# Attention scores in two float32r terms, and exponentials over three PSUM banks, in a convolution-and-attention kernel

## The chip, the core and the metric

The kernel runs on one core of a Trainium2 chip. The core has five engines that this text names: TensorE (PE in the profile; PEld is its weight load), VectorE (DVE), ScalarE (ACT), GpSimd (POOL) and SyncE (SP), which here only issues DMAs. Matmuls write to PSUM, which has eight banks of 512 float32 columns on 128 partitions; the other engines work from SBUF and PSUM.

The metric is device time in microseconds (us) of one execution. Before the change it is 10433.82 us, the median of three runs (10430.26 to 10446.56).

## What is computed

Two layers are applied to four images of 64 x 64 pixels with 128 channels. The part that matters here is the attention of the second layer ("layer 1"): per image 4096 tokens, 16 heads of 8 channels, no mask.

```python
q = (x @ wq).reshape(bsz, seqlen, N_HEADS, HEAD_DIM)
k = (x @ wk).reshape(bsz, seqlen, N_HEADS, HEAD_DIM)
v = (x @ wv).reshape(bsz, seqlen, N_HEADS, HEAD_DIM)
scores = jnp.einsum('bqhd,bkhd->bhqk', q, k)
probs = jax.nn.softmax(scores.astype(jnp.float32), axis=-1).astype(q.dtype)
attn = jnp.einsum('bhqk,bkhd->bqhd', probs, v).reshape(bsz, seqlen, DIM)
h = x + attn @ wo
```

Around it stand, in layer 0, two 3 x 3 convolutions and a causal attention with one small head, and after it in layer 1 a gated feed-forward network and a mixture of eight experts. All of it is float32, and the scores must keep nearly float32 accuracy.

## The kernel before

The four images are done one after another (L681). For each: convolutions (`l0_convs`), layer 0's attention (`l0_attention`), the transposed input `yT`, `l1_attention`, then `l1_ffn` and `l1_experts` over eight blocks of 512 tokens.

**Layer 1's attention** (L430 to L564) is written by hand in the order in which TensorE is to do it; the tile framework puts in the waits. It has two parts.

*Preparation* (L435 to L464). For each of eight column blocks of 512 tokens two matmuls make the queries and the keys in one PSUM tile. `three_terms` (L234) splits these float32 numbers into three bfloat16 terms whose sum is the number: ScalarE rounds the first term (L238), VectorE takes the rest (L239), GpSimd rounds the second (L240), VectorE takes the third (L241). The terms go out to DRAM (L444, L445), since they must come back in another order of partitions. Values `v1` are made at L453 to L463.

*The main loop* (L517 to L563). Heads are done in four groups `g` of four heads; a head has its own group ("slot") of 32 SBUF partitions. For each group and each block `c` of 512 queries (128 such pairs over the four images) there are 32 tiles `kt` of 128 keys. For each key tile:

- Scores (L546). The keys `kx` lie with 8 channels x 3 terms = 24 rows in each slot, and the queries `qx` hold, for each query term i, that term repeated on the 24 rows. So three matmuls of 24 rows, added up in PSUM, give all nine products of terms. Four heads times three terms are 12 matmuls, for four banks: two score tiles `s` of 1024 columns. There are three such tiles (L103), in six banks.
- Exponentials (L556). ScalarE turns each score tile into an SBUF tile `e` of 1024 columns, from a pool of eight.
- Accumulation (L509), two key tiles late (`LAG`). For each head one float32 matmul of a 128 x 9 weight (a one for the softmax's sum, and 8 value channels) adds to `acc`, the head's 32 partitions of one further bank. The trace records each of these float32 matmuls as two.

After the last key tile VectorE copies `acc` to SBUF (L524), and in the next block, after its second key tile, `by_token` transposes and divides it (L495 to L500); the transposes have the eighth bank.

Keys are loaded for a whole group (L474) into one of two buffers, queries for a block (L483) into one of two, both one ahead. All these DMAs are issued by SP in program order.

The pools that the change touches serve other stages too: the score tiles and `e` tiles are used by the convolutions, layer 0's attention (scores L402, exponentials L415 and L418, accumulation L381), the feed-forward network (L583 to L587) and the experts (L666, L675).

Of the kernel before, what the change touches and what calls it, by code (L numbers as in the profile page):

```python
# [8 lines left out]

FP = mybir.dt.float32  # L10
BF = mybir.dt.bfloat16
AF = mybir.ActivationFunctionType
ALU = mybir.AluOpType
AX = mybir.AxisListType

P = 128
C = 128
IMG = 64
N = IMG * IMG
NT = N // P  # L20
QB = 512
NQ = N // QB
# [4 lines left out]
SLOT = 32  # L27
NSLOT = P // SLOT
# [5 lines left out]
HIDDEN = 344  # L34
FCH = [(0, 128), (128, 128), (256, 88)]
NE = 8

NTERM = 3  # L40
# [49 lines left out]
def fast_path(ctx: ExitStack, tc: tile.TileContext, a: dict, where: dict, out: bass.AP, verdict):  # L90
# [2 lines left out]
    x = a["x"]  # L93
    B = x.shape[0]
    LAG = 2

    const = ctx.enter_context(tc.tile_pool(name="f_const", bufs=1))
    big = ctx.enter_context(tc.tile_pool(name="f_big", bufs=1))
    ep = ctx.enter_context(tc.tile_pool(name="f_ep", bufs=8))
    wk = ctx.enter_context(tc.tile_pool(name="f_wk", bufs=2))  # L100
    sm = ctx.enter_context(tc.tile_pool(name="f_sm", bufs=2))
    dram = ctx.enter_context(tc.tile_pool(name="f_dram", bufs=2, space=bass.MemoryType.DRAM))
    ps_s = ctx.enter_context(tc.tile_pool(name="f_ps_s", bufs=3, space=bass.MemoryType.PSUM))  # L103
    ps_o = ctx.enter_context(tc.tile_pool(name="f_ps_o", bufs=1, space=bass.MemoryType.PSUM))
    ps_m = ctx.enter_context(tc.tile_pool(name="f_ps_m", bufs=1, space=bass.MemoryType.PSUM))

    def s_tile():
        return ps_s.tile([P, 1024], FP, tag="s", name="s")

    def m_tile():  # L110
        return ps_m.tile([P, QB], FP, tag="m", name="m")

    def e_tile():
        return ep.tile([P, 1024], FP, tag="e", name="e")


    n_fast = where["head_sum"][1]
# [311 lines left out]

    def l1_attention(b, yT, h):  # L430

        d_k = dram.tile([P, NTERM, N], BF, tag="k1", name="d_k1")
        d_q = dram.tile([NQ, P, NTERM, QB], BF, tag="q1", name="d_q1")
        top = sm.tile([P, 2, NQ], FP, tag="top", name="top")
        for c in range(NQ):  # L435
            cols = slice(c * QB, (c + 1) * QB)
            ps = s_tile()
            nc.tensor.matmul(ps[:, :QB], lhsT=wq1, rhs=yT[:, cols], start=True, stop=True)
            nc.tensor.matmul(ps[:, QB:], lhsT=wk1, rhs=yT[:, cols], start=True, stop=True)
            nc.vector.tensor_reduce(  # L440
                top[:, :, c], ps.rearrange("p (j n) -> p j n", j=2), AX.X, ALU.max, apply_absolute_value=True
            )
            terms = three_terms(ps)
            nc.sync.dma_start(out=d_k[:, :, cols], in_=terms[:, :, QB:])  # L444
            nc.sync.dma_start(out=d_q[c], in_=terms[:, :, :QB])  # L445

        tops = sm.tile([P, 2], FP, tag="tops", name="tops")
        nc.vector.tensor_reduce(tops, top, AX.X, ALU.max)
        nc.vector.tensor_tensor(seen[:, 2, b : b + 1], tops[:, 0:1], tops[:, 1:2], ALU.mult)
        nc.vector.tensor_scalar(seen[:, 2, b : b + 1], seen[:, 2, b : b + 1], 1e30, None, ALU.min)  # L450

# [12 lines left out]
        nc.vector.tensor_reduce(seen[:, 3, b : b + 1], top_v, AX.X, ALU.max)  # L464


        rows = HD1 * NTERM

        def keys(g):
            kx = big.tile([P, N], BF, tag="kx", bufs=2, name="kx")  # L470
            for j in range(NSLOT):
                head = NSLOT * g + j
                src = d_k[head * HD1 : (head + 1) * HD1].rearrange("d y n -> (d y) n")
                nc.sync.dma_start(out=kx[j * SLOT : j * SLOT + rows, :], in_=src)  # L474
            return kx

        def queries(g, c):

            qx = wk.tile([P, NTERM, QB], BF, tag="qx", name="qx")
            for j in range(NSLOT):  # L480
                head = NSLOT * g + j
                src = d_q[c][head * HD1 : (head + 1) * HD1].rearrange("d x n -> d (x n)")
                nc.sync.dma_start(  # L483
                    out=qx[j * SLOT : j * SLOT + rows].rearrange("p x n -> p (x n)"),
                    in_=src.unsqueeze(1).to_broadcast([HD1, NTERM, NTERM * QB]),
                )
            return qx

        nt = big.tile([P, NT, C], FP, tag="y", name="nt")

        def by_token(g, c, at):

            ps = m_tile()
            for k in range(4):
                nc.tensor.transpose(ps[:, k * P : (k + 1) * P], at[:, k * P : (k + 1) * P], ident)  # L495
# [11 lines left out]
        def add_up(g, c, kt, es):  # L507
            for j in range(NSLOT):
                nc.tensor.matmul(  # L509
                    acc[j * SLOT : j * SLOT + 1 + HD1, :],  # L510
                    lhsT=v1[:, kt, NSLOT * g + j, :],
                    rhs=es[j // 2][:, (j % 2) * QB : (j % 2 + 1) * QB],
                    start=kt == 0,
                    stop=kt == NT - 1,
                )

        order = [(g, c) for g in range(NG1) for c in range(NQ)]  # L517
        ready = []

        def finish(n, kt, es):  # L520
            add_up(*order[n], kt, es)
# [7 lines left out]
        kx, qx = keys(0), queries(0, 0)  # L529
        kx_next = qx_next = None  # L530
        late = []
        for n, (g, c) in enumerate(order):
            if n:
                qx = qx_next
                if c == 0:
                    kx = kx_next
            if n + 1 < len(order):
                qx_next = queries(*order[n + 1])
            if c == 0 and g + 1 < NG1:
                kx_next = keys(g + 1)  # L540
            for kt in range(NT):
                ss = [s_tile(), s_tile()]
                for i in range(NTERM):
                    for j in range(NSLOT):
                        r = slice(j * SLOT, j * SLOT + rows)
                        nc.tensor.matmul(  # L546
                            ss[j // 2][:, (j % 2) * QB : (j % 2 + 1) * QB],
                            lhsT=kx[r, kt * P : (kt + 1) * P],
                            rhs=qx[r, i, :],
                            start=i == 0,  # L550
                            stop=i == NTERM - 1,
                        )
                es = []
                for ps in ss:
                    e = e_tile()
                    nc.scalar.activation(e, ps, AF.Exp)  # L556
                    es.append(e)
                late.append((n, kt, es))
                if len(late) > LAG:
                    finish(*late.pop(0))  # L560
        for item in late:
            finish(*item)
        by_token(*order[-1], ready.pop())  # L563
        return nt  # L564

# [847 lines left out]
```

## Time and profile before

| | |
|---|---|
| median of three runs | 10433.82 us |
| the profiled execution | 10433.93 us |
| its span, first to last instruction | 10432.1 us |
| mean granted TensorE clock | 0.966 |
| TensorE busy | 9972.6 us (96%) |
| ScalarE busy | 8198.4 us (79%) |
| VectorE busy | 1150.2 us (11%) |
| GpSimd busy | 184.3 us (2%) |

The profile is one execution taken by the hardware profiler. In its list of costliest groups a row gives the line, engine and operation, what is written from what, the shapes and the count; then the busy time in all, the mean time of one in ns, and the idle time of the engine just before them with what ended it. Busy time counts overlapping instructions of an engine once, so a group's busy time can be less than its count times its mean. Ends of matmuls are modelled, and a busy TensorE may be one that waits. The chain of waits follows the work that ended last backwards, from each instruction to what released it. A table of stretches gives, for each stretch, the busy time and count of each engine, the granted clock, and the DMA share and rate. A timeline lists start, length, engine, line and count of merged instructions.

### The profile page before, as it was taken

The numbers are of one execution on the slowest core, as the hardware profiler recorded it, in microseconds if no ns is written. First come the engines' busy times: TensorE is split into PE (matmuls) and PEld (weight loads), VectorE is DVE, ScalarE is ACT, GpSimd is POOL, SyncE is SP. The second block draws the span as 40 slices with busy tenths as digits, with TensorE's granted clock in tenths as the row PEclk, the third lists the DMA queues.
The fourth block names the chain that finished last, engine by engine and source line by source line (L and its number), as shares of the span: only waits on it lengthen the run. The fifth ranks groups of instructions, "written<-read, shape, count | busy, mean of one in ns | idle before, by whom it ended". The sixth has DMA issues, their size and how long they took to land.

```text
span 10432.1 us, 204188 instructions
## 1 busy us (share of the span) xinstructions
PE 9972.6 (96%) x90561; PEld 3179.9 (30%) x90565; DVE 1150.2 (11%) x3539; ACT 8198.4 (79%) x8965; POOL 184.3 (2%) x177
## 2 busy tenths in 40 slices
PE   8899999997989999999798999999979899999997
PEld 4322222224432222222442222222244222222224
DVE  1200000004220000000412000000051200000005
ACT  1699999991169999999116999999911799999991
POOL 0000000000000000000000000000000000000000
PEclk9999999998999999999889999999988999999998
DMA  1100000000010000000001000000000100000000
GB/s 26 35 6 10 6 9 7 6 5 15 5 34 6 10 6 9 7 6 5 16 4 35 7 9 6 10 6 6 5 16 4 35 7 9 6 10 6 6 5 9
DMA packets 86914, 112.51 MB, mean 11 GB/s; under 512 B 8835, under 2 KB 71779, under 8 KB 84195
## 3 DMA queue, kind: packets, MB, share of 16 engines
q1 hardware_dynamic: 83267, 97.59, 3.2%
q8 instruction: 710, 11.63, 0.5%
q10 hardware_dynamic: 2752, 1.77, 0.1%
q14 instruction: 185, 1.52, 0.0%
HBM read 64.99 MB, written 34.34 MB: 10 GB/s over the span
## 4 chain that ended last, share of the span: by engine, by line
PE 93%; DVE 4%; DMA 1%; ACT 1%; issue 0%; SPq 0%; POOL 0%; DVEq 0%; ACTq 0%; POOLq 0%
PE acc L509 38%; PE s L546 35%; PE s L291 5%; PE s L276 2%; PE s L666 2%; PE acc L381 2%; DVE t L675 2%; PE s L402 1%; PE s L583 1%; PE s L584 1%; PE m L495 1%; PE m L592 1%; PE m L231 1%; PE s L367 1%; PE m L574 0%
## 5 line engine op out<-in xcount | busy, mean ns | idle before, releaser
L556 ACT ACTIVATE e<-s 128x1024 f32<-128x1024 f32 x8192 | 7642.7, 1022 | 149.5 <-PE s L546 149.5
L509 PE MATMUL acc<-e,f_v 128*9 128x512 f32 x32768 | 4296.2, 595 | 4.5 <-ACT e L556 4.5
L546 PE MATMUL s<-qx,kx 24*128 24x512 bf16 x49152 | 3926.0, 377 | 29.5 <-DMA kx<-d_k 28.5
L546 PEld LDWEIGHTS <-kx 24*128 24x128 bf16 x49152 | 1548.0, 91 | 3823.5 <-issue 3467.2
L509 PEld LDWEIGHTS acc<-e,f_v 128*9 128x9 f32 x32768 | 486.7, 88 | 1753.4 <-issue 1687.1
L524 DVE COPY at<-acc 128x512 f32<-128x512 f32 x128 | 88.6, 692 | 7149.6 <-PE acc L509 7149.6
L291 PE MATMUL s<-c,f_w2c 128*128 128x512 f32 x1152 | 499.9, 592 | 0.0
L666 PE MATMUL s<-f_we,e 128*128 128x512 f32 x512 | 313.1, 763 | 58.2 <-DVE t L675 53.2
L299 ACT ACTIVATE e<-s,f_b 128x512 f32<-128x512 f32 x32 | 22.0, 687 | 422.8 <-PE s L291 422.7
L675 DVE SCALAR_TENSOR_TENSOR t<-s,gate,t 128x128 f32<-128x128 f32 x1024 | 305.9, 343 | 5.3 <-PE s L666 2.5
L291 PEld LDWEIGHTS s<-c,f_w2c 128*128 128x128 f32 x1152 | 215.5, 189 | 263.5 <-issue 263.5
L418 ACT ACTIVATE e<-s 128x1024 f32<-128x1024 f32 x224 | 217.6, 1021 | 91.1 <-PE s L402 90.4
L276 PE MATMUL s<-e,f_w1c 128*128 128x512 f32 x576 | 249.9, 596 | 3.1 <-DVE t L675 1.9
L402 PE MATMUL s<-qk 36*128 36x512 bf16 (+1 forms) x576 | 169.3, 388 | 76.0 <-DMA qk<-d_q 74.1
L655 ACT COPY g<-m 8x512 f32<-8x512 f32 x32 | 18.4, 575 | 230.4 <-PE m L653 230.4
L232 ACT COPY e<-m 128x512 f32<-128x512 f32 x64 | 37.5, 586 | 204.4 <-PE m L231 204.4
L381 PE MATMUL acc<-e,f_v 128*17 128x512 f32 (+3 forms) x1152 | 197.7, 600 | 0.0
L586 ACT ACTIVATE e<-s 128x512 f32<-128x512 f32 (+1 forms) x96 | 56.8, 596 | 165.6 <-PE s L584 165.5
L588 POOL TENSOR_TENSOR t<-t,h 128x512 f32<-128x512 f32 x32 | 40.5, 1266 | 8117.7 <-DVE h L577 8117.7
L666 PEld LDWEIGHTS s<-f_we,e 128*128 128x128 f32 x512 | 118.7, 247 | 202.9 <-issue 120.9
L283 ACT ACTIVATE c<-s,f_b 128x1024 f32<-128x1024 f32 x16 | 17.9, 1118 | 186.7 <-PE s L276 186.7
L276 PEld LDWEIGHTS s<-e,f_w1c 128*128 128x128 f32 x576 | 109.2, 190 | 141.7 <-issue 141.0
(146 smaller groups left out, 2962.0 us busy)
## 6 DMA issues: line engine op xcount, KB each, us to landing
qx<-d_q SPq DMA_DIRECT2D x512, 72.0 KB
d_k<-x SPq DMA_DIRECT2D x32, 384.0 KB
d_q<-x SPq DMA_DIRECT2D x32, 384.0 KB
kx<-d_k SPq DMA_DIRECT2D x64, 192.0 KB
t<-in_x_dram SPq DMA_DIRECT2D x16, 512.0 KB
out_dram<-t SPq DMA_DIRECT2D x32, 256.0 KB
f_w2c<-in_L_conv_W_dram ACTq DMA_DIRECT2D x1, 1152.0 KB
qk<-d_q SPq DMA_DIRECT2D x12, 96.0 KB
```

Of the source, the lines that this page charges most:

```text
L231: nc.tensor.transpose(ps[:, k * P : (k + 1) * P], src[:, k, :], ident)
L276: nc.tensor.matmul(rows(ps[:, h * QB : (h + 1) * QB]), lhsT=w1c[:, tap, :], rhs=e0[:, r0 : r0 + 8, kx : kx + IMG], start=(tap == 0), stop= ...
L291: nc.tensor.matmul(rows(ps[:, h * QB : (h + 1) * QB]), lhsT=w2c[:, tap, h * C : (h + 1) * C], rhs=c1[:, 8 * c + ky : 8 * c + ky + 8, kx : ...
L367: nc.tensor.matmul(ps[:, k * C : (k + 1) * C], lhsT=l_, rhs=w3f, start=True, stop=True)
L381: nc.tensor.matmul(acc[j * SLOT : j * SLOT + 1 + DV0, off:], lhsT=v0[:, kt, :], rhs=e[:, lo:hi], start=r == 0, stop=r == c,)
L402: nc.tensor.matmul(ps[:, lo:hi], lhsT=kx[:kr, kt * P : (kt + 1) * P], rhs=qx[:kr, c * QB + off : (c + 1) * QB], start=True, stop=r < c,)
L418: nc.scalar.activation(e, ps, AF.Exp)
L509: nc.tensor.matmul(acc[j * SLOT : j * SLOT + 1 + HD1, :], lhsT=v1[:, kt, NSLOT * g + j, :], rhs=es[j // 2][:, (j % 2) * QB : (j % 2 + 1) * ...
L546: nc.tensor.matmul(ss[j // 2][:, (j % 2) * QB : (j % 2 + 1) * QB], lhsT=kx[r, kt * P : (kt + 1) * P], rhs=qx[r, i, :], start=i == 0, stop= ...
L556: nc.scalar.activation(e, ps, AF.Exp)
L666: nc.tensor.matmul(px[:, h * QB : (h + 1) * QB], lhsT=yT[:, k * P : (k + 1) * P], rhs=we_f[:, h * QB : (h + 1) * QB], start=True, stop=True,)
L675: nc.vector.scalar_tensor_tensor(tk, px[:, n * C : (n + 1) * C], gate[:, k, n : n + 1], tk, ALU.mult, ALU.add)
```

## The change

The scores are made from two float32r terms instead of three bfloat16 terms. float32r is a four-byte type of the matmul; the first term is the number as ScalarE writes it in that type, the second is the rest. Two key terms times two query terms times 8 channels are 32 rows, a whole slot, so one matmul for each head and key tile gives all four products, where three were added up before. The keys now come back from DRAM by four DMAs, one for each quarter of the keys, each of all four heads, into one buffer instead of two. The queries come by one DMA for each block; for this, each column block's query terms are written to DRAM twice.

The two score tiles now have three banks each (1536 columns), and an exponential covers three banks. The (block, key tile, head) triples of an image form one list that is handed out three at a time, without regard to where a key tile ends; a step is three score matmuls and one exponential. The accumulation of a key tile is called when its fourth head comes up, with a lag of two steps. There are five `e` tiles of 1536 columns instead of eight of 1024. Other stages get the same tiles and use 1024 columns of them.

```diff
+FR = mybir.dt.float32r
...
+    WIDE = 3
...
-    ep = ctx.enter_context(tc.tile_pool(name="f_ep", bufs=8))
+    ep = ctx.enter_context(tc.tile_pool(name="f_ep", bufs=5))
...
-    ps_s = ctx.enter_context(tc.tile_pool(name="f_ps_s", bufs=3, space=bass.MemoryType.PSUM))
+    ps_s = ctx.enter_context(tc.tile_pool(name="f_ps_s", bufs=2, space=bass.MemoryType.PSUM))
...
-    def s_tile():
-        return ps_s.tile([P, 1024], FP, tag="s", name="s")
+    def s_tile(n=2):
+        return ps_s.tile([P, WIDE * QB], FP, tag="s", name="s")[:, : n * QB]
...
-        d_k = dram.tile([P, NTERM, N], BF, tag="k1", name="d_k1")
-        d_q = dram.tile([NQ, P, NTERM, QB], BF, tag="q1", name="d_q1")
+        d_k = dram.tile([P, 2, N], FP, tag="k1", name="d_k1")
+        d_q = dram.tile([NQ, P, 2, 2, QB], FP, tag="q1", name="d_q1")
...
-            terms = three_terms(ps)
+            terms = wk.tile([P, 2, 1024], FP, tag="x", name="two")
+            nc.scalar.copy(terms[:, 0, :].bitcast(FR), ps)
+            nc.vector.tensor_tensor(terms[:, 1, :].bitcast(FR), ps, terms[:, 0, :], ALU.subtract)
             nc.sync.dma_start(out=d_k[:, :, cols], in_=terms[:, :, QB:])
-            nc.sync.dma_start(out=d_q[c], in_=terms[:, :, :QB])
+            for y in range(2):
+                nc.sync.dma_start(out=d_q[c][:, y], in_=terms[:, :, :QB])
...
+        kx = big.tile([P, N], FP, tag="kx", bufs=1, name="kx")
+
         def keys(g):
...
+            src = d_k[g * SLOT : (g + 1) * SLOT].rearrange("d y n -> (d y) n")
+            for s in range(4):
+                cols = slice(s * N // 4, (s + 1) * N // 4)
+                nc.sync.dma_start(
+                    out=kx[:, cols], in_=src[:, cols].unsqueeze(1).to_broadcast([2 * SLOT, 2, N // 4])
+                )
 
         def queries(g, c):
...
+            qx = wk.tile([P, QB], FP, tag="qx", name="qx")
+            nc.sync.dma_start(out=qx, in_=d_q[c][g * SLOT : (g + 1) * SLOT].rearrange("d y x n -> (d y x) n"))
             return qx
...
+        work = [(n, kt, j) for n in range(len(order)) for kt in range(NT) for j in range(NSLOT)]
+        late, qx, qx_next = [], None, queries(0, 0)
+        have = {}
+        keys(0)
+        for first in range(0, len(work), WIDE):
+            now = work[first : first + WIDE]
+            ps = s_tile(WIDE)
+            for i, (n, kt, j) in enumerate(now):
+                if kt == 0 and j == 0:
+                    qx = qx_next
+                    if n + 1 < len(order):
+                        qx_next = queries(*order[n + 1])
+                r = slice(j * SLOT, (j + 1) * SLOT)
+                nc.tensor.matmul(
+                    ps[:, i * QB : (i + 1) * QB],
+                    lhsT=kx[r, kt * P : (kt + 1) * P].bitcast(FR),
+                    rhs=qx[r, :].bitcast(FR),
+                    start=True,
+                    stop=True,
+                )
+                g, c = order[n]
+                if c == NQ - 1 and kt == NT - 1 and j == NSLOT - 1 and g + 1 < NG1:
+                    keys(g + 1)
+            e = ep.tile([P, WIDE * QB], FP, tag="e", name="e")
+            nc.scalar.activation(e[:, : len(now) * QB], ps[:, : len(now) * QB], AF.Exp)
+            late.append([(w, e[:, i * QB : (i + 1) * QB]) for i, w in enumerate(now)])
+            if len(late) > LAG:
+                late_now = late.pop(0)
+            else:
+                late_now = []
+            if first + WIDE >= len(work):
+                late_now += [w for ws in late for w in ws]
+            for (n, kt, j), part in late_now:
+                have[j] = part
+                if j == NSLOT - 1:
+                    add_up(n, kt, have)
```

More of the change, by code (lines that the diff above doesn't have):

```diff
@@ L113, in e_tile @@
     def e_tile():
-        return ep.tile([P, 1024], FP, tag="e", name="e")
+        return ep.tile([P, WIDE * QB], FP, tag="e", name="e")[:, :1024]
     n_fast = where["head_sum"][1]
@@ L464, in l1_attention @@
         nc.vector.tensor_reduce(seen[:, 3, b : b + 1], top_v, AX.X, ALU.max)
-        rows = HD1 * NTERM
+        kx = big.tile([P, N], FP, tag="kx", bufs=1, name="kx")
         def keys(g):
[L470 to L475, printed above, removed]
-        def queries(g, c):
[L479 to L486, printed above, removed]
+            src = d_k[g * SLOT : (g + 1) * SLOT].rearrange("d y n -> (d y) n")
[4 more added lines that the diff above has]
+                )
+        def queries(g, c):
+            qx = wk.tile([P, QB], FP, tag="qx", name="qx")
+            nc.sync.dma_start(out=qx, in_=d_q[c][g * SLOT : (g + 1) * SLOT].rearrange("d y x n -> (d y x) n"))
             return qx
@@ L505, in by_token, with add_up @@
             )
-        def add_up(g, c, kt, es):
+        order = [(g, c) for g in range(NG1) for c in range(NQ)]
+        ready = []
+        def add_up(n, kt, es):
+            g, c = order[n]
             for j in range(NSLOT):
@@ L511, in add_up @@
                     lhsT=v1[:, kt, NSLOT * g + j, :],
-                    rhs=es[j // 2][:, (j % 2) * QB : (j % 2 + 1) * QB],
+                    rhs=es[j],
                     start=kt == 0,
@@ L515, in add_up @@
                 )
[L517 to L521, printed above, removed]
             if kt == NT - 1:
@@ L527, in finish @@
                 by_token(*order[n - 1], ready.pop())
[L529 to L560, printed above, removed]
@@ L561, in l1_attention @@
-        for item in late:
-            finish(*item)
+        work = [(n, kt, j) for n in range(len(order)) for kt in range(NT) for j in range(NSLOT)]
[18 more added lines that the diff above has]
+                )
+                g, c = order[n]
+                if c == NQ - 1 and kt == NT - 1 and j == NSLOT - 1 and g + 1 < NG1:
[13 more added lines that the diff above has]
+                    add_up(n, kt, have)
```

## The prediction

> **What bounds the kernel now.** I began with the page (engine shares and costliest groups), then asked where the two score lines run.
>
> ```profile
> PE 9972.6 (96%) x90561; PEld 3179.9 (30%) x90565; DVE 1150.2 (11%) x3539; ACT 8198.4 (79%) x8965; POOL 184.3 (2%) x177
> ...
> L556 ACT ACTIVATE e<-s 128x1024 f32<-128x1024 f32 x8192 | 7642.7, 1022 | 149.5 <-PE s L546 149.5
> L509 PE MATMUL acc<-e,f_v 128*9 128x512 f32 x32768 | 4296.2, 595 | 4.5 <-ACT e L556 4.5
> L546 PE MATMUL s<-qx,kx 24*128 24x512 bf16 x49152 | 3926.0, 377 | 29.5 <-DMA kx<-d_k 28.5
> ```
>
> L556, the exponential of layer 1's attention, fills 7642.7 + 149.5 = 7792 us: three quarters of the span, and the stage that the change rewrites. Of its idle time the first two waits of a batch (15.22 and 3.80 us in ScalarE's timeline of the first batch; 76 us for four batches) belong to the start of the stage, so the stage itself is about 7716 us. Which engine sets its pace? The table of stretches says both:
>
> ```profile
> 700.00:800.00 100.00, 100.00 (x1076) 27.07 (x1068) 2.48 (x6) 98.97 (x107) 0.00 (x0) 1.00 0.03 7
> ```
>
> PE 100.00, ACT 98.97 of 100 us, clock 1.00. The chain of waits names PE throughout, but look at one change of query block:
>
> ```profile
> 1511.21 0.98 PE acc L509 x8
> 1512.19 0.85 PE s L546 x12
> 1513.05 1.01 PE acc L509 x8
> 1514.05 0.89 PE s L546 x12
> 1514.94 0.98 PE acc L509 x8
> 1515.92 0.59 PE m L495 x4
> 1516.51 0.76 PE s L546 x12
> 1517.26 0.98 PE acc L509 x8
> ```
>
> Twelve score matmuls take 0.85 to 0.92 us everywhere, but 0.76 just after the 0.59 us of transposes, when ScalarE had run ahead and every score tile was free. So PE alone needs 0.76 + 0.975 = 1.735 us for a key tile and is held to about 1.87 by score tiles that ScalarE has not yet read. **ScalarE is the bound, and PE is 7% behind it.** Any gain on ScalarE is soon used up on PE.
>
> **ScalarE's part of the change.** Each exponential covers 1536 columns instead of 1024. Rows: 1022 ns at 1024 columns (L556) and 597 ns at 512 (L586), so 0.83 ns a column and 1447 ns at 1536. The busy time per instruction, 7642.7 / 8192 = 933 ns, is less than 1022: neighbours overlap by about 90 to 100 ns. So a step costs about 1.35 us. There are 4 x 1366 = 5464 steps: **7376 us** against 7716.
>
> **PE's part.** The changed program's instruction order on TensorE shows 5332 stretches of score matmuls (nearly all of three) and 5332 stretches of accumulation. The loop text suggests accumulation in three steps of four; the order shows the four matmuls of every third key tile split into one and three, with scores between. The eight records of a stretch are four matmuls of two halves, and the four run side by side in 0.98 us. One alone has the same two halves in sequence, so I charge 0.975 for every stretch: the split costs one extra stretch in four steps.
>
> A score stretch is now three float32r matmuls of 32 rows, which this trace does not show. What it does show: in the quiet stretch above, TensorE's timeline has score matmuls starting in fours, about 0.22 us apart (1516.44, then 1516.88 two rounds later). Twelve in 0.76 is three rounds of four, so one round with the drain at its end is 0.76 - 2 x 0.22 = about 0.31 to 0.32. Four matmuls on the same rows take longer:
>
> ```profile
> 316.99 0.97 PE s L402 x4
> 317.96 0.98 PE acc L381 x8
> ```
>
> so different row groups do run side by side. What four-byte weights add is seen where they come first after other work:
>
> ```profile
> 365.73 1.10 PE L438 MATMUL s<-yT,f_wq 128*128 128x512 f32 x2
> 366.67 1.02 PE L439 MATMUL s<-yT,f_wk 128*128 128x512 f32 x2
> 367.53 1.02 PE L438 MATMUL s<-yT,f_wq 128*128 128x512 f32 x2
> ```
>
> 1.10 against 1.02: 0.08 us of load not hidden. The bounds: per stretch, below 0.31 (bf16, load hidden) is excluded, as the columns must still pass; above, three whole f32 matmuls in turn, 3 x 0.868 + 0.18 = 2.8. I take one pass at the bf16 rate, side by side, plus the 0.08: **0.39 us**, because a 32-row group is nearest to L546 and its weights nearest to L438.
>
> [...]
>
> Sum for PE: 5332 x (0.975 + 0.39) = 7278; the 132 triples that stand in longer stretches, 132 x 0.22 = 29. At each of 128 query blocks the transposes add 0.59. There the accumulator must also be copied first: the copy starts 0.07 us after the scores and lasts 0.69 (1512.26, L524), and the next accumulation starts 0.86 after the scores did. Scores of 0.85 hid that; scores of 0.39 leave 0.47, and the next scores are queued behind that wait. 128 x (0.59 + 0.47) = 136. Together **7443 us**, just above ScalarE's 7376, so PE is late next. The stage gains 7716 - 7443 = 273 us.
>
> **What lies beside it.** Score tiles go from three to two, of three banks each. In the new loop ScalarE reads 1.35 us while PE refills the other tile in about 0.4 plus latency, so the refill is covered; the price without cover is inside the bounds above. In layer 0's attention two tiles of 1024 are tight: PE's cycle is 0.97 + 0.98 = 1.95, the second tile's scores would start 0.43 us into it, while its last reader ends some 0.3 later; spread over two tiles about 0.16 for each of 112 full blocks, plus up to 0.3 at 32 diagonal ones: +28 (bounds 0 and 100). Five exponential buffers still exceed the steps in flight: nothing.
> The split into terms loses a DVE pass (1220 ns, L241) and a POOL pass (1039 ns, L240) for each of 32 column blocks, but writes 1536 KB instead of 768. ScalarE already waits there for x buffers to be written out (69.1 us, "DMA d_q<-x"). DVE is busy 42 of 55 us in that stretch, so the bounds are -40 and +64; I take 0.
> Keys now have one buffer. The order shows four DMAs, each waiting for the last scores on its own quarter, so three quarters land during the last block of the group and the last has 24 key tiles (over 40 us) before use; landing took 5 us at the start (issue 413.82, last wait over 418). Nothing; if all four waited for the end, 12 x 6 = 72. The query DMAs queued behind them on SP are issued a block ahead.
>
> Total: -273 + 28 = -245. The profiled execution took 10433.9 (span 10432.1 and 1.8 around it), the same as the median 10433.8. **10433.9 - 245 = 10189, say 10190.**
>
> **Rivals.**
> 1. *Row groups do not run side by side in float32r* (slower). Then a stretch is 2 x 0.216 longer, 0.82: 5332 x 0.43 = +2300, 12490. For it: no four-byte matmul here has 32 rows, and L402 shows what turns cost. Against: 24-row groups (L546) and f32 column groups (L509) both overlap. It decides from a stretch of 0.39 + 245 / 5332 = 0.436 us: PE has only 0.046 us to spare.
> 2. *A pass takes two cycles a column*, as one half of an f32 matmul does (0.434 for L291): 5464 x 0.216 = +1180, 11370. *As four passes*, no float32r gain at all: +3500, 13700.
> 3. *The weight load is exposed in full*, 0.19: +590, 10780. Between 0.12 and 0.13 exposed, no change.
> 4. *Weights hidden as for bf16*: PE falls to 7016 and ScalarE bounds: 7376, and with the -40 above 10080 to 10120.
>
> **Chances.** Forecast and rival 4: 0.50 (10080 to 10410). No change: 0.06. Weights exposed: 0.12 (10460 to 11000). Two cycles: 0.12 (to 11400). In turn: 0.12. Four passes: 0.08. The range leaves out the last two: 10080 to 11400; the forecast's own is 10080 to 10410. About 0.2% (21 us) is what a measurement can tell from no change: faster 0.50, same 0.06, slower 0.44.
>
> **What would show it.** Right: exponentials of about 1447 ns, score stretches near 0.39 in the chain with starts of three a few ns apart, accumulation at 0.98, ScalarE at 97 to 99%. Wrong: score starts 0.2 us apart (rival 1), stretches of 0.6 or more (2), 0.5 (3), or ScalarE idle at "DMA kx" at group changes. Accumulation of one taking less than 0.98 would make it faster than I say.

## The result, and the profile after

The changed kernel takes 10533.6 us (median of four runs, 10515.7 to 10541.8) against 10439.0 of the kernel before in the same session (10430.3 to 10446.6): a ratio of 1.0089, 95% interval 1.0071 to 1.0106. It is slower by 0.9%; the forecast was 10190.

The profiled execution of the changed kernel is the fastest of its four, 10515.7 us, with a span of 10513.9. First its page, the shares and the groups that answer to those shown of before (busy us, mean ns of one, idle time and its releaser):

```profile
PE 9943.9 (95%) x57797; PEld 2750.3 (26%) x57797; DVE 1135.7 (11%) x3507; ACT 8154.0 (78%) x6237; POOL 151.1 (1%) x145
...
L550 ACT ACTIVATE e<-s 128x1536 f32<-128x1536 f32 x5464 | 7587.4, 1463 | 192.6 <-PE s L539 192.5
L512 PE MATMUL acc<-e,f_v 128*9 128x512 f32 x32768 | 5554.6, 595 | 46.9 <-DVE at L521 46.9
L539 PE MATMUL s<-qx,kx 32*128 32x512 f32 x16384 | 2738.9, 495 | 48.6 <-ACT e L550 37.7
L539 PEld LDWEIGHTS s<-qx,kx 32*128 32x128 f32 x16384 | 1023.8, 181 | 4571.8 <-ACT e L550 4276.1
```

The exponentials are as long as computed (1463 ns against an estimate of 1447), and the score matmuls keep TensorE busy for 2739 us in place of 3926. But accumulation has grown from 4296 to 5555 us with the same number of matmuls, each at the same 595 ns: what has changed is how many of them lie side by side. The last row shows how a releaser can mislead. It says that the score weights wait 4276 us for exponentials, yet TensorE is accumulating during that time: the weight load at 1501.41 shows a wait of 0.86 us, and an accumulation has run since 1500.44. The load stands ahead of its matmul and carries that matmul's wait. The chain of waits decides:

```profile
1500.51 0.97 PE acc L512 x6
1501.48 0.44 PE s L539 x3
1501.92 0.98 PE acc L512 x8
1502.89 0.43 PE s L539 x2
1503.32 0.98 PE acc L512 x8
1504.30 0.44 PE s L539 x2
1504.74 0.96 PE acc L512 x2
1505.70 0.43 PE s L539 x2
```

The chain of waits in the main loop is TensorE alone. Accumulations of three, four, four and one matmul (six, eight, eight and two records) all take 0.96 to 0.98 us, and between any two stands a score stretch of 0.43 to 0.44. In the table of stretches, 700 to 800 us (the stretch that was shown of before; PE, PEld, DVE, ACT, POOL, then the clock):

```profile
700.00:800.00 100.00, 98.66 (x647) 21.68 (x644) 2.48 (x6) 98.14 (x72) 0.00 (x0) 1.00 0.02 6
```

Here ACT's 98% is a trap. 72 exponentials take 100 us, 1390 ns each, and in the runs below in which ScalarE sets the pace a step takes 1347. So some 40 ns of each are waiting that the profile counts as busy. Both engines look full, and only the chain says which leads.

By stages, summed over the four images (profile against profile): the layer-1 main loop, first exponential to last accumulation, went from 7736 to 7716 us; the layer-0 attention from 465 to 590; everything else together became 24 us shorter. That is the 82 us between the two profiles. The change bought almost nothing where it was made and paid where nothing was rewritten. The layer-0 attention of the four images in the changed kernel:

```profile
251.19:407.18 155.99, 148.27 (x620) 43.09 (x621) 33.30 (x141) 75.14 (x96) 7.07 (x7) 0.83 0.00 1
2877.51:3014.90 137.39, 129.54 (x620) 39.34 (x621) 33.30 (x141) 75.03 (x96) 7.06 (x7) 0.96 0.00 1
5484.53:5632.95 148.42, 140.82 (x620) 41.11 (x621) 33.30 (x141) 75.13 (x96) 7.06 (x7) 0.88 0.00 1
8112.96:8261.23 148.27, 140.67 (x620) 41.11 (x621) 33.30 (x141) 75.11 (x96) 7.06 (x7) 0.88 0.00 1
```

and two of those before:

```profile
249.61:365.73 116.12, 113.20 (x620) 40.70 (x621) 33.29 (x141) 72.27 (x96) 7.07 (x7) 0.89 0.00 1
2853.78:2969.98 116.20, 113.28 (x619) 40.78 (x621) 33.29 (x141) 72.27 (x96) 7.06 (x7) 0.89 0.00 1
```

The instructions are the same (620 matmul records), each stage is 21 to 40 us longer, and the clock explains little of it: the second image is 21 us longer at a higher clock, 0.96 against 0.89. In the instruction order of the two kernels the accumulations of this attention stand in 172 stretches before and 264 after. With two score tiles in place of three the scheduler moves accumulations in between the scores here too. The prediction had looked at that order only in the main loop.

A part of the chain in the first of these, where an accumulation of four is split into one (x2) and three (x6):

```profile
344.56 0.53 issue
345.10 1.03 ACT e L421
346.17 0.59 PE s L370 x2
...
354.16 1.82 PE acc L384 x2
355.97 0.96 PE s L405 x2
356.94 1.83 PE acc L384 x6
...
367.90 0.97 PE acc L384 x6
```

TensorE waits for an exponential ahead of the projection (L370), which needs a score tile when both are held; soon after, an accumulation takes 1.82 us, and 0.97 again at 367.9. For these 20 us the clock is at half.

### The profile page after: what moved, and what is told of

Read it like the earlier page. It is cut to its first block, busy times and chain, and to the rows that moved or that the text cites. A ratio compares the mean times of both kernels' runs of the same rounds, so it can differ in the third digit from the quotient of the medians.

```text
span 10513.9 us, 132704 instructions
## 1 busy us (share of the span) xinstructions
PE 9943.9 (95%) x57797; PEld 2750.3 (26%) x57797; DVE 1135.7 (11%) x3507; ACT 8154.0 (78%) x6237; POOL 151.1 (1%) x145
## 4 chain that ended last, share of the span: by engine, by line
PE 89%; DVE 4%; ACT 4%; issue 1%; DMA 1%; SPq 0%; POOL 0%; ACTq 0%; DVEq 0%; POOLq 0%
PE acc L512 48%; PE s L539 21%; PE s L294 5%; PE s L279 2%; ACT e L550 2%; PE s L665 2%; PE acc L384 2%; PE s L405 1%; DVE t L674 1%; PE s L582 1%; DVE at L521 1%; PE s L583 1%; PE m L494 1%; PE m L591 1%; PE m L234 1%
## 5 line engine op out<-in xcount | busy, mean ns | idle before, releaser
L550 ACT ACTIVATE e<-s 128x1536 f32<-128x1536 f32 x5464 | 7587.4, 1463 | 192.6 <-PE s L539 192.5
L512 PE MATMUL acc<-e,f_v 128*9 128x512 f32 x32768 | 5554.6, 595 | 46.9 <-DVE at L521 46.9
L539 PE MATMUL s<-qx,kx 32*128 32x512 f32 x16384 | 2738.9, 495 | 48.6 <-ACT e L550 37.7
L539 PEld LDWEIGHTS s<-qx,kx 32*128 32x128 f32 x16384 | 1023.8, 181 | 4571.8 <-ACT e L550 4276.1
L512 PEld LDWEIGHTS acc<-e,f_v 128*9 128x9 f32 x32768 | 601.5, 88 | 1371.2 <-issue 1283.0
L421 ACT ACTIVATE e<-s 128x1024 f32<-128x1024 f32 x224 | 224.8, 1023 | 173.6 <-PE s L405 173.1
L665 PE MATMUL s<-f_we,e 128*128 128x512 f32 x512 | 290.7, 703 | 71.7 <-DVE t L674 68.9
L384 PE MATMUL acc<-e,f_v 128*17 128x512 f32 (+3 forms) x1152 | 295.6, 622 | 0.0
L405 PE MATMUL s<-qk 36*128 36x512 bf16 (+2 forms) x576 | 185.9, 400 | 82.4 <-DMA qk<-d_q 74.5
```

The source lines that it names most:

```text
L384: nc.tensor.matmul(acc[j * SLOT : j * SLOT + 1 + DV0, off:], lhsT=v0[:, kt, :], rhs=e[:, lo:hi], start=r == 0, stop=r == c,)
L405: nc.tensor.matmul(ps[:, lo:hi], lhsT=kx[:kr, kt * P : (kt + 1) * P], rhs=qx[:kr, c * QB + off : (c + 1) * QB], start=True, stop=r < c,)
L512: nc.tensor.matmul(acc[j * SLOT : j * SLOT + 1 + HD1, :], lhsT=v1[:, kt, NSLOT * g + j, :], rhs=es[j], start=kt == 0, stop=kt == NT - 1,)
L539: nc.tensor.matmul(ps[:, i * QB : (i + 1) * QB], lhsT=kx[r, kt * P : (kt + 1) * P].bitcast(FR), rhs=qx[r, :].bitcast(FR), start=True, stop ...
L550: nc.scalar.activation(e[:, : len(now) * QB], ps[:, : len(now) * QB], AF.Exp)
L665: nc.tensor.matmul(px[:, h * QB : (h + 1) * QB], lhsT=yT[:, k * P : (k + 1) * P], rhs=we_f[:, h * QB : (h + 1) * QB], start=True, stop=True,)
```

## The experiments

**Theory 1**: TensorE sets the pace of the changed loop. It pays 0.96 us for each of the 1240 accumulation stretches that the scheduler split off, and a score stretch of 0.43 in place of the forecast 0.39, because more of the four-byte weight load is exposed. **Rival**: the two score tiles hand over too slowly between TensorE and ScalarE, whatever the order. For the layer-0 attention, **theory A**: two score tiles there cost the time, by splits or by waits that hold TensorE's clock at half; its rival, that something else did, is stated with each run.

**Main loop in the program's order.** The framework can pin a matmul behind the one traced before it:

```diff
-                nc.tensor.matmul(
+                tc.keep_in_program_order(nc.tensor.matmul(
                     acc[j * SLOT : j * SLOT + 1 + HD1, :],
```

and likewise for the scores of the loop (L539).

> The main loop of layer 1's attention is held to the order of its source on TensorE (each score or accumulation matmul behind the one traced before it), so that the four accumulations of a key tile stand together: 4092 stretches of accumulation instead of 5332. Theory 1 (TensorE's own stretches set the pace: 0.44 us of scores and 0.97 us of accumulation, whether of one, three or four matmuls): TensorE needs 4092 x (0.975 + 0.44) + 1372 x 0.22 + 128 x 0.59 = 6.17 ms, below ScalarE's 5464 x 1.34 = 7.32 ms, so ScalarE bounds; the stage falls from 7716 to between 7330 and 7450 us and the kernel to between 10150 and 10270 us. Theory 2 (the handover of two score tiles sets the pace: each score stretch waits for ScalarE's release of its tile): the handover is the same, and the time stays within 50 us of 10534.

Measured: 10205.7 us (10199.8 to 10217.6), ratio to the kernel before 0.9787 [0.9771, 0.9804]; loop 7393 us, layer-0 attention 598. Another order of the same instructions is worth about 3%. In the table of stretches ScalarE is now hardly idle and TensorE has slack:

```profile
3000.00:3500.00 500.00, 441.73 (x3362) 105.48 (x3358) 10.62 (x25) 498.29 (x371) 0.00 (x0) 1.00 0.03 10
```

371 exponentials in 500 us are 1348 ns each, the 1.35 us a step of the forecast. So the handover theory falls.

**Layer-0 attention in the program's order.** The same pinning of L384, L405 and L415 alone.

> Only layer 0's attention is held to the order of its source on TensorE; the main loop of layer 1 is left as changed. Its accumulations then stand in 140 stretches instead of 264 (172 before the change). Theory 1 (split accumulation stretches, about 1 us each, made layer 0's attention 125 us longer): 590 us falls by 90 to 125 us, and the kernel to between 10400 and 10450 us. Theory 2 (two score tiles instead of three make TensorE and ScalarE wait for each other there, whatever the order): a gain of at most 30 us, 10500 or more.

Measured: 10703.9 us (10697.8 to 10709.5), 1.0265 [1.0247, 1.0282]: a miss, and in the other direction. The main loop is unchanged (7715), the layer-0 attention has gone to 776 us, though its accumulations now stand in only 140 stretches. Two of its four images:

```profile
250.06:449.18 199.12, 175.09 (x619) 54.57 (x621) 33.28 (x141) 75.12 (x96) 7.07 (x7) 0.50 0.00 1
2925.94:3115.36 189.42, 165.14 (x619) 49.29 (x621) 33.28 (x141) 74.92 (x96) 7.06 (x7) 0.54 0.00 1
```

The granted clock is 0.50 nearly throughout. In TensorE's timeline (the bracket is the idle time just before, and its releaser) the waits recur at the scores, the diagonal blocks and the projections:

```profile
323.19 1.01 PE L405 MATMUL s<-qk 36*128 36x512 bf16 x2 [1.17 <-ACT e L421]
...
337.34 0.26 PE L405 MATMUL s<-qk 36*128 36x128 bf16 x1 [0.53 <-ACT e L418]
...
344.23 0.77 PE L370 MATMUL s<-f_w3f,at 128*128 128x128 f32 x2 [0.93 <-DVE at L366]
```

**Two bf16 terms.** The changed kernel with bfloat16 in place of float32r, which leaves the third term out.

```diff
-            terms = wk.tile([P, 2, 1024], FP, tag="x", name="two")
+            terms = wk.tile([P, 2, 1024], BF, tag="x", name="two")
```

and so for the tiles and DMAs behind it.

> The changed kernel with bfloat16 in place of float32r for the two terms; the third term of the numbers is left out, so that the scores are less exact. The instruction order on TensorE is the same as the changed kernel's, 5332 stretches of each kind. Theory 1 (a four-byte weight load that nothing hides costs about 0.12 us a stretch): score stretches fall from 0.44 to 0.31 to 0.33 us, TensorE's step from 1.42 to 1.29 us, below ScalarE's 1.34; the stage falls to between 7320 and 7480 us and the kernel to between 10150 and 10310 us. Theory 2 (handover): no change in the stage, 10480 or more. If the moving operand were the cost and not the load, the spacing of the matmuls would change with the type, too.

Measured: 10136.1 us (10111.4 to 10147.6), 0.9712 [0.9690, 0.9733]; loop 7381. Its order is that of the changed kernel, split accumulations included, so the 336 us of the loop come from two-byte in place of four-byte operands alone. Here ScalarE is the bound:

```profile
3000.00:3500.00 500.00, 493.20 (x3376) 96.74 (x3368) 11.17 (x27) 498.47 (x371) 0.00 (x0) 1.00 0.02 5
```

As with the pinned order, 371 exponentials fill 498 of 500 us, so most score stretches contain a wait for ScalarE and take 0.35 us or more. Of 5200 stretches of three, 392 did not wait and took 0.32 to 0.33; in the changed kernel none took less than 0.425 and the median is 0.433. **So four-byte operands add 0.10 to 0.11 us per stretch**, not 0.08. The forecast's 0.31 to 0.32 for a stretch without that was about right.

This run changes weights and columns together. That it is the weights shows in the changed kernel itself, in the 40 stretches of six that wait for nothing. In one of them TensorE's timeline has the first three matmuls and the last two:

```profile
590.71 0.50 PE L539 MATMUL s<-qx,kx 32*128 32x512 f32 x3
...
591.05 0.40 PE L539 MATMUL s<-qx,kx 32*128 32x512 f32 x2
```

The weights of the last two are loaded from 590.83 on, some 0.2 us ahead of them. These two take 0.39 us each by the trace, where the first three take 0.49 to 0.50; bf16 has 0.37 to 0.385. The accumulation starts 0.32 us after them, as in bf16. So four-byte columns cost nothing more, and only a load that nothing hides does, once in a stretch.

The loads themselves are recorded at 181 ns in float32r and 91 in bf16, and no row here isolates the part that is exposed; 0.10 to 0.11 is the difference of the two runs. The prediction took the 0.08 of a row at L438. With 0.10 to 0.11 in its place the forecast would have been about 10300 to 10350 (5332 x 0.02 to 0.03 more), still about 200 us short of what was measured.

**float32r alone.** The kernel before with the two float32r terms, three score tiles of 1024, the old loop and the old exponentials.

```diff
+                        lhsT=kx[r, kt * P : (kt + 1) * P].bitcast(FR),
+                        rhs=qx[r, :].bitcast(FR),
```

> Only the float32r half of the change: the old loop with three score tiles of two banks and exponentials of 1024 columns, four float32r matmuls in place of twelve bfloat16 ones, keys in one buffer. Theory 1: TensorE needs 0.44 + 0.975 us for a key tile, well below ScalarE's two exponentials of 0.915 us; ScalarE bounds at 8192 x 0.915 = 7500 us plus little at the ends of query blocks; layer 0's attention, whose order is that of before, is back at 465 us; the kernel is between 10190 and 10280 us, faster than before. Rival (float32r matmuls are the loss in themselves): 10439 us or more.

Measured: 10212.4 us (10202.8 to 10244.6), 0.9798 [0.9774, 0.9822]; loop 7533, layer-0 attention 475. Half of the change, without the wide exponentials, gives 2.0%.

**Six banks as one tile.** To give the layer-0 attention three tiles of two banks again and the loop two of three, one tile of six banks was cut into slices:

```diff
+    six = ps_s.tile([P, 6 * QB], FP, tag="s", name="s")
+        k = turn[n] = (turn.get(n, -1) + 1) % (6 // n)
+        return six[:, k * n * QB : (k + 1) * n * QB]
```

with both attentions pinned in the first kernel, the main loop alone in the second.

> The six score banks become one tile, cut into three slices of two banks wherever 1024 columns are asked for and into two slices of three in the layer-1 loop, and the order of the program is kept on TensorE in both attentions (140 accumulation stretches in the layer-0 attention, 4092 in the layer-1 loop). Theory A (the layer-0 attention became longer because with two score tiles TensorE waits for exponentials, its busy share falls, and its clock stays at half): with three slices the layer-0 attention is back at 460 to 490 us from the 776 of the same order with two tiles, the layer-1 loop stays at about 7393, and the whole is 10060 to 10110 us. Theory B (the number of tiles doesn't matter there; it was the order): the layer-0 attention stays at 590 to 780 us and the whole at 10200 to 10390.

> As the kernel with three slices, but the layer-0 attention in the scheduler's own order, which splits its accumulations into 348 stretches (172 in the kernel before, 264 in the changed one). Theory A1 (a split accumulation costs a whole one, 0.96 us, here too): 176 stretches more than in the kernel before, 0.169 ms, so the layer-0 attention at 620 to 650 us, and its clock full after the first part. Theory A2 (only the waits for score tiles and the clock that they cost count, and extra stretches are hidden): 465 to 490 us.

Measured: 17091 us, 1.638 [1.635, 1.641], and 16976 us in one run: the test missed its object. In the timeline scores and exponentials now take turns:

```profile
3002.21 0.80 PE L543 MATMUL s<-qx,kx 32*128 32x512 f32 x3 [1.63 <-ACT e L554]
...
3003.11 1.45 ACT L554 ACTIVATE e<-s 128x1536 f32<-128x1536 f32 x1 [0.96 <-PE s L543]
3004.76 0.29 PEld L543 LDWEIGHTS s<-qx,kx 32*128 32x128 f32 x3 [1.70 <-ACT e L554]
3004.76 0.80 PE L543 MATMUL s<-qx,kx 32*128 32x512 f32 x3
```

Scores start only 0.2 us after an exponential of the other slice has ended. So slices of one tile are no double buffer here; the waits follow the whole tile. The mean clock is 0.674 with TensorE busy 76%. On the layer-0 attention these two runs say nothing.

**Scores of the layer-0 attention twice.** In the kernel with that attention pinned, each score matmul is issued a second time and overwrites its own result.

> The changed kernel with the program's order kept in the layer-0 attention (776 us there, TensorE at half clock nearly throughout), and every score matmul of the layer-0 attention issued twice, the first result overwritten by the second: 576 matmuls more, which take at least 0.216 us each at the full clock, 0.125 ms. Theory A (the clock stays at half because TensorE waits part of the time): the added work fills the waits, the clock rises to full, and the layer-0 attention becomes shorter in spite of it, 590 to 680 us. Theory B (the clock does not follow the waits): the added work comes on top at half clock, 0.25 ms, and the layer-0 attention takes 950 to 1050 us.

Measured: 10910 us (one run); that attention 950 us, 174 more than before, at the lower edge of theory B. TensorE is busy 95% in this stretch, and still gets half the clock:

```profile
300.00:350.00 50.00, 47.62 (x162) 15.62 (x160) 9.32 (x40) 15.81 (x19) 2.02 (x2) 0.50 0.00 0
```

But the added work did not go where the longest waits are: in its timeline 0.93 us remain ahead of each projection (for VectorE's copy of the accumulator) and 0.53 in each diagonal block. So a busy share of 95% does not by itself bring the full clock; whether the short waits keep it away is taken up again in the last run.

**Wide exponentials alone.** Three bf16 terms, with the exponentials over three banks and the hand-out across steps.

```diff
+            for i3 in range(NTERM):
+                for i, kt, r, kx_, qx_ in step:
+                    nc.tensor.matmul(
+                        ps[:, i * QB : (i + 1) * QB],
```

> The three bf16 terms of the kernel before, with exponentials over three banks, two score tiles and the hand-out across steps. Its score stretches are 2728 of nine matmuls and 1360 of eighteen, its accumulations 4084 stretches of four (so the scheduler splits none here). In the kernel before the step of 1.889 us holds 0.976 us of accumulation and so 0.91 us of twelve score matmuls in three groups of four side by side. Three side by side take the same three group times, so a stretch of nine costs 0.85 to 0.91 us and one of eighteen 1.5 to 1.8. Theory 1 (TensorE sets the time): layer-1 loop 4084 x 0.976 + 2728 x 0.88 + 1360 x 1.65 = 8630 us (8300 to 8950), and with the layer-0 attention longer by about 125 the whole at 11100 to 11800. Rival (ScalarE sets the time of the loop once its exponentials are wide): loop at 7400 to 7700, the whole at 10200 to 10500.

Measured: 10986 us (one run), loop 8156, layer-0 attention 609. TensorE sets the time (ScalarE's exponentials idle 577 us ahead of them, 539 of it for scores), as theory 1 said. Its number was too high (8300 at least) since a stretch of nine takes 0.75 us, not 0.88, and one of eighteen about 1.45, not 1.65: the 0.85 to 0.92 of twelve in the kernel before held waits for score tiles, and without them it was 0.76. Alone, this half of the change loses 5%.

**Score banks handed out anew.** Pools opened and closed around the loop, so that each stage has tiles of its own width:

```diff
+    def cut(n):
+        held.close()
+        name = "f_ps_s%d" % len(cur)
+        cur.append(held.enter_context(tc.tile_pool(name=name, bufs=6 // n, space=bass.MemoryType.PSUM)))
...
+        cut(WIDE)
         for first in range(0, len(work), WIDE):
```

and `cut(2)` behind the loop. In the first kernel nothing is pinned, in the second the main loop.

> The changed kernel, with the score banks of the program handed out anew before and after each layer-1 loop: three tiles of two banks everywhere else, two of three banks in the loop. Nothing is pinned; the accumulations of the layer-0 attention then stand in 172 stretches, as in the kernel before, those of the layer-1 loop in 5332, as in the changed kernel. Theory A (the longer layer-0 attention of the changed kernel comes of having two score tiles there: split accumulations, waits and a lower clock): the layer-0 attention is back at 460 to 485 us from 590, the layer-1 loop stays at 7716, and the whole is 10380 to 10430 us, about what the kernel before takes. Rival (the layer-0 attention became longer through something else that the change brought, the state of the clock on entering it for one): it stays at 560 to 600 us and the whole at 10490 to 10540.

> As the kernel before this in the list, and the program's order kept on TensorE in the layer-1 loop alone (4092 accumulation stretches there, 172 in the layer-0 attention). If the two losses are independent they add up: loop 7393 as with the order alone, layer-0 attention 460 to 485, the whole 10205.7 - 130 = 10060 to 10110 us, 0.963 to 0.969 of the kernel before. Rival (ScalarE sets the time of the loop already and the layer-0 attention does not come back): 10190 to 10230.

Measured: 10377.5 us (10358.4 to 10388.1), 0.9945 [0.9930, 0.9961], with the layer-0 attention at 463 and the loop at 7715; and **10052.6 us** (10039.3 to 10065.4), **0.9639 [0.9625, 0.9652]**, with 475 and 7395. Two images of the layer-0 attention of the first:

```profile
249.30:363.34 114.04, 110.87 (x620) 39.76 (x621) 33.29 (x141) 72.25 (x96) 7.07 (x7) 0.91 0.00 1
2824.06:2940.30 116.24, 113.32 (x619) 40.84 (x621) 33.29 (x141) 72.31 (x96) 7.06 (x7) 0.89 0.00 1
```

These are the lengths of the kernel before. So the two score tiles are the cause of the longer layer-0 attention, by order, waits and clock together, and the two losses add up: 328 us for the order of the loop and 156 for the tiles (127 of them in that attention), taken from 10533.6, leave 10050. The second kernel beats both. ScalarE bounds its loop:

```profile
L560 ACT ACTIVATE e<-s 128x1536 f32<-128x1536 f32 x5464 | 7358.7, 1653 | 92.2 <-PE s L549 90.7
L521 PE MATMUL acc<-e,f_v 128*9 128x512 f32 x32768 | 4292.7, 596 | 32.1 <-DVE at L530 32.1
```

The accumulation is back at 4293 us, and 7358.7 / 5464 is 1347 ns a step.

**Plain float32 scores.** The changed kernel without the two casts to float32r at L541 and L542.

> The changed kernel with the score matmuls in plain float32 in place of float32r (the same terms, so the products are at least as exact). If plain float32 takes four passes of 0.216 us where float32r takes one, a score stretch of three is 0.65 us longer, 1.05 to 1.10 us, and one of six 1.9 to 2.4; its accumulations stand in 4092 stretches here, so the loop is 4092 x 0.976 + 2724 x 1.08 + 1360 x 2.1 = 9800 us (9400 to 10300) and the whole 12200 to 13200. If it took one pass the loop would be at 7400 and the whole at 10200 to 10300.

Measured: 12415 us (one run), loop 9603. A stretch of three is recorded as six matmuls in two halves 0.53 us apart and takes 1.064 us, against 0.433. The difference of 0.63 us is about three times the 0.22 us by which the rounds of score matmuls follow each other in the kernel before, near the 0.65 of the expectation. Its four passes for one are an estimate that fits; the trace does not show single passes. Three such matmuls in turn would take 2.6 us by the forecast's bound (3 x 0.868), so the row groups run side by side here too.

**Both attentions in order, three tiles.** The pinned order of the layer-0 attention that took 776 us with two tiles, now with three.

> The kernel with three score tiles outside the layer-1 loop and two of three banks in it, with the program's order kept on TensorE in both attentions: the order of the layer-0 attention (140 accumulation stretches) that took 776 us with two score tiles, now with three. Theory A (two tiles make TensorE wait at the projections and diagonal blocks, and the waits hold its clock at half): with three the layer-0 attention takes 450 to 490 us at the full clock after its first part, and the whole 10030 to 10080. Rival (it was the pinned order itself that left TensorE waiting, above all for the copy of the accumulator ahead of each projection): it takes 700 to 790 us at half clock, and the whole 10280 to 10380.

Measured: 10261.7 us (10235.0 to 10294.5), 0.9845 [0.9820, 0.9870]; that attention 622 us, between the two theories. Two of its images:

```profile
249.38:392.50 143.12, 129.34 (x621) 46.05 (x621) 33.30 (x141) 73.29 (x96) 7.08 (x7) 0.71 0.00 1
5323.10:5491.65 168.55, 154.93 (x620) 52.05 (x621) 33.30 (x141) 73.78 (x96) 7.06 (x7) 0.58 0.00 1
```

and what still waits, in TensorE's timeline:

```profile
305.85 0.21 PE L414 MATMUL s<-qk 36*128 36x128 bf16 x1 [0.54 <-ACT e L427]
...
310.00 0.49 PE L379 MATMUL s<-f_w3f,at 128*128 128x128 f32 x2 [0.86 <-DVE at L375]
```

So of the 314 us that the pinned order with two tiles loses against the 463 of three tiles and a free order, about half (155) belongs to the tiles and half (159) to the pinning, which leaves the copy ahead of each projection uncovered (waits of 0.86 us there, where three tiles and a free order have 0.27). Multiply each image's length by its clock and the pinned order is no more work than the order before (about 400 us over four images in either pinned kernel, 414 before): by this measure, what it loses, it loses to the clock. In the changed kernel itself that product is 522, so there it seems to be mostly more work (92 extra stretches x 0.96 = 88 us of the 109) and only some 16 us of clock. The product is a rough measure, since the waits for other engines keep about their length: in a diagonal block 0.53 us at half clock with two tiles and 0.54 at the full clock with three, ahead of a projection 0.93 and 0.86.

## Why the prediction was wrong

The steps, in its own order, profile against profile:

- **ScalarE, 1.35 us a step, 7376 in all: right.** 1347 ns a step where it bounds (7393 and 7395 for the loop).
- **Accumulation, 0.975 for every stretch, split or not: right.** 0.957, 0.970 and 0.975 for one, three and four matmuls; 5332 stretches.
- **One pass, at the bf16 rate, side by side: right.** The three start within 7 ns of each other, a matmul whose load is covered takes 0.39 against 0.37 to 0.385 in bf16, and plain float32 costs 0.63 more a stretch. Rivals 1 and 2 fall.
- **"0.39 us" for a score stretch: this is the step that failed.** It measured 0.433. Its base of 0.31 to 0.32 held; the exposed weight load that was added to it was 0.08, from a row of two float32 matmuls on all 128 rows at L438, and is 0.10 to 0.11. 5332 x 0.043 = 229 us of the 273 by which the loop, 7716 us, is longer than the 7443 forecast. Rival 1 had named the margin, 0.046, and rival 3 put "no change" at 0.12 to 0.13 exposed (its 0.19 for a load in full is the mean of L291's float32 weight loads in the profile before, 189 ns): the measured loop, 20 us better than before, lies just there. A term with 5332 repeats and so little margin deserved more than the 0.12 that its rival was given.
- **Copy of the accumulator at each block, 0.47: right.** At 124 block changes the next accumulation starts 0.87 to 0.89 us after the scores do, where the forecast had 0.39 + 0.47 = 0.86. One of them in TensorE's timeline:

```profile
706.80 0.50 PE L539 MATMUL s<-qx,kx 32*128 32x512 f32 x3
707.68 0.62 PE L512 MATMUL acc<-e,f_v 128*9 128x512 f32 x4 [0.38 <-DVE at L521]
```

- **The triples in longer stretches, 29 us: too small.** 0.22 each holds for 40 stretches of six, which take 0.66 us. In 84 others the second three wait until ScalarE has read their tile, and the stretch takes 1.12 to 1.14; 84 x 0.47 = about 40 us. One of these:

```profile
833.41 0.50 PE L539 MATMUL s<-qx,kx 32*128 32x512 f32 x3
...
834.11 0.50 PE L539 MATMUL s<-qx,kx 32*128 32x512 f32 x3 [0.20 <-ACT e L550]
```

- **The loop before, 7716: too small by 20.** From the first exponential to the last accumulation it took 7736.
- **Layer 0's attention, "+28 (bounds 0 and 100)": failed, value and bound.** It lost 125. The step reckoned the waits for tiles in the old order, and did not ask what the scheduler would do with two tiles there; the order of the changed program shows 264 stretches for 172.
- **The split into terms, keys and `e` buffers, 0: right.** From the first query and key matmul to the first exponential, 214 before and 215 after.

Sum: 229 + 40 + 97 (the layer-0 attention, 125 for 28) - 20 (the loop before) - 24 (other stages) = 322, beside 10515.7 - 10190 = 326. The two terms that lessen the miss were not foreseen; they are luck.

The rest of the reasoning held: TensorE became late next. The prediction's larger omission is one of questions: it saw that the order splits the accumulations, charged it (1240 x 0.975 = 1209 us of TensorE's time), and did not list it as the first thing that a kernel near the balance of two engines can't afford.

What stays open: the 125 us in the changed kernel's layer-0 attention were not split by a run into extra stretches and clock; the 88 and 16 above are worked out from counts and clocks. The number of stretches alone does not set that time: 140 in pinned order took 622 us with three tiles, 172 in the scheduler's order 463.

## What to carry to other kernels

When a change moves work off one engine, compare the two engines' new paces before anything else: here 0.975 + 0.43 stood against 1.35, and an error of 0.04 us in a term repeated 5332 times took the gain. A price that appears once per switch, as the exposed weight load (0.10 to 0.11 us here) and the accumulation of one to four matmuls (0.96 to 0.98) do, is multiplied by the number of switches, so read the instruction order of every stage that shares the changed buffers, and where the scheduler splits a group, pin it. Measure each pinning, though: it gained 328 us in the loop, where ScalarE then led, and lost 186 in the layer-0 attention with two tiles and 159 with three.

## What the runs showed of the hardware beyond that

- In these records the granted clock is either full (1.00) or half (0.50). In the changed kernel's first layer-0 attention it falls at 325.9 and at 346.4, each time within 3 us of a wait of 0.91 us ahead of a projection (the waits end at 323.2 and 346.2), while shorter waits there, of 0.19 to 0.54 us, bring no fall. It then stays at half for 6.8 and for 20.5 us; in the second stretch TensorE is busy throughout:

```profile
346.36:366.84 20.48, 20.48 (x58) 5.29 (x57) 3.96 (x19) 6.85 (x7) 1.01 (x1) 0.50 0.00 1
```

In the kernel before, a wait of 0.83 us ends at 260.4, and the clock is full 15 us later. But in the last run two waits of 0.86 us, which end at 310.0 and 324.6, lie in a stretch at the full clock:

```profile
304.48:338.62 34.14, 30.22 (x197) 10.92 (x197) 9.32 (x40) 23.23 (x32) 2.02 (x2) 1.00 0.00 0
```

So no length of wait that brings the clock down follows from these traces. The rise took 20.5 us of work without a stop in the stretch from 346.36, and the clock fell with no idle time above 0.91 us near. That waits cause the fall is argued from where they stand; no run here added or removed a single one.
- The same 416 matmuls of the feed-forward network took 118.2 us at a clock of 1.00 and 136.5 at 0.82, in two images of one kernel (the first with score banks handed out anew). In the changed kernel this stage is 35 us shorter than before over the four images, at a higher clock; that is more than the 24 us by which the other stages together became shorter, and none of it is put down to the change.
